# One more half of x convolved on VectorE, and the means of squares on TensorE without column quarters: a change to a convolution, state-space and recurrence kernel

## The chip, the cores and the metric

The kernel runs on one core of one Trainium2 chip. The metric is the device time of one launch in microseconds (us). Before the change three timed runs took 3141.71, 3144.81 and 3148.75 us; the median, 3144.81 us, is the time before. The engines are named as the profile names them: PE is TensorE's matmul, PEld its weight load, DVE is VectorE, ACT is ScalarE, POOL is GpSimd and SP is SyncE, whose queue issues most of the transfers. Each engine works through its own instructions in order.

## The reference, cut to what matters

There are two layers. The first is a group norm, three convolutions and an attention over pixels; the second is a state-space block in two directions over the 4096 tokens of each of four images, followed by a normalized recurrence. The change touches only the state-space block. Cut to that block:

```python
def _mamba3(x, in_proj, conv_w, conv_b, A_log, dt_bias, D, norm_w, out_proj):   # once forwards, once backwards
    zxbcdt = x @ in_proj                                   # 128 channels in
    z, xbc, dt = jnp.split(zxbcdt, [D_INNER, D_INNER + CONV_DIM], axis=-1)   # D_INNER = 256
    xp = jnp.pad(xbc, ((0, 0), (K - 1, 0), (0, 0)))        # K = 4 taps
    conv = sum((xp[:, i:i + l, :] * conv_w[:, i] for i in range(K))) + conv_b
    xbc = jax.nn.silu(conv)
    xh, Bm, Cm = jnp.split(xbc, [D_INNER, D_INNER + D_STATE], axis=-1)
    ...                                                    # dt = softplus(...), A = -exp(A_log)
    y = _ssd(xh, dt, A, Bm, Cm) + xh * D[None, None, :, None]   # chunked scan
    yg = y.reshape(b, l, D_INNER) * jax.nn.silu(z)
    yn = yg * jax.lax.rsqrt(jnp.mean(yg * yg, -1, keepdims=True) + EPS) * norm_w
    return yn @ out_proj
```

So `x` has 256 channels in each of two directions: four halves of 128 channels. Each half needs a projection, a causal convolution over four taps along the tokens, a bias and a SiLU.

## The kernel before

Channels lie on the 128 partitions and tokens along the columns. A *step* n is a chunk of 128 tokens in each direction; four steps make a *group* of 512 tokens; eight groups make an image (a *sequence*), and there are four images: 128 steps, 32 groups. While group G is scanned, the projections of group G+1 are made in between. The instructions of PE and of ACT stand in the order in which the program writes them; those of DVE and POOL are ordered by a scheduler.

A half of x comes about in one of two ways. One projection, then the four taps on ACT (the first) and DVE (the other three):

```python
def project(gr, i, c):                        # direction i, half c
    px = ring.tile([P, MG], F32, tag="big", name="px")       # PSUM, a ring of 3 buffers
    wx = w[1]["x"][:, bass.ts(c, P)] if i else w[0]["x1"]
    nc.tensor.matmul(px, wx, tl[:, rows(g, i, PAD)], start=True, stop=True)              # L1124
    ...
    nc.vector.memset(...)                                                                 # L1128
    nc.scalar.activation(at(0), px, AF.Identity, scale=taps[:, PAD:KC], bias=...)         # L1129
    if g:
        ...  nc.vector.tensor_tensor(v, v, past ..., ALU.add)      # 3 columns, L1133
    for n in range(1, KC):
        nc.vector.scalar_tensor_tensor(at(n), px, taps[...], at(n), ALU.mult, ALU.add)    # L1135

def activate(gr, i, c):
    nc.scalar.activation(x, x, AF.Silu)                                                   # L1139
```

Or four projections, one for each tap with weights that have the tap multiplied in, accumulated in PSUM; only the first half of the forward direction is made so:

```python
def project_fwd(gr):
    px = ring.tile([P, MG], F32, tag="big", name="px")
    for tap in range(KC):
        nc.tensor.matmul(px, w[0]["x"][:, tap, :], tl[:, rows(g, 0, tap)], start=(tap == 0), stop=(tap == KC - 1))  # L1115
    nc.scalar.activation(gr["x"][0][:, 0, :], px, AF.Silu, bias=w[0]["cb"][:, 0:1])       # L1116
```

The means of squares over 256 channels, for the norm at the end, go to two quarters of the array's columns:

```python
def means(gr):                                # QT = 32
    pm = ring.tile([ND * QT, MG], F32, tag="big", name="pm")
    for d in range(ND):
        nc.tensor.matmul(pm[bass.ts(d, QT)], mean, gr["z"][d][:, 0, :], start=True, stop=True,
                         tile_position=(0, d * QT))                                       # L1283
    ms = wk.tile([ND * QT, MG], F32, tag="row", name="ms", bufs=3)
    nc.vector.tensor_scalar(ms, pm, RMS_EPS, None, ALU.add)                               # L1287
    ...
    nc.sync.dma_start(m1..., ms[::QT])        # out to memory, back as columns, rsqrt, spread again
```

One step of the loop, cut to its order (`states` L1212 and L1224, `turn` L1177, `scan` L1234 and L1242, `prepare` L1187 to L1202, `differences` L1168):

```python
for n in range(N):
    G, j = divmod(n, MT)                      # j: 0 to 3 within the group
    S1 = states(m[n], S)                      # PE small L1212, DVE S L1224
    turn(m[n + 1])                            # PE ptr L1177
    scan(m.pop(n), y, S)                      # PE y L1234, L1242
    prepare(m[n + 1])     # PE small L1187, L1189; ACT Exp L1191, copy bt L1193; DVE L1196, gm L1200, lt L1201
    if n % 2: take(gr, j, y)                  # DVE yT L1254
    if j == 0:
        open_group(G + 1); squares(groups[G - 1])
        project(groups[G + 1], 1, 0); project_bc(groups[G + 1], 0); project(groups[G + 1], 0, 1)
    elif j == 1:
        means(groups[G - 1])
        project(groups[G + 1], 1, 1); project_bc(groups[G + 1], 1)     # pb L1103, SiLU L1107
    elif j == 2:
        project_fwd(groups[G + 1])
        for i, c in ((1, 0), (0, 1), (1, 1)): activate(groups[G + 1], i, c)
        for i in range(ND):
            for c in range(2): project_z(gr, i, c)                      # pz L1146, SiLU L1147
        gate(gr, 1)
    elif j == 3:
        gate(gr, 3); back(groups.pop(G - 1))                            # po L1308
    differences(m[n + 2])                     # ACT Relu, 8 times, L1168
    # and, in some steps, pieces of the next image's opening and of the last image's statistics (ls_in L83)
```

Of the kernel before, what the change touches and what calls it, by code (L numbers as in the profile page):

```python
# [10 lines left out]
F32 = mybir.dt.float32  # L11
AF = mybir.ActivationFunctionType
ALU = mybir.AluOpType
# [3 lines left out]
P = 128  # L17
# [9 lines left out]
DS = 64  # L27
DI = NHEAD * HD
KC = 4
GT = NC // P  # L30
DIRS = ("fwd", "bwd")
MG = 512
# [855 lines left out]
def mamba(nc, tc, k, a, t, B, T, vec, first=None, after=None, mr=None):  # L888
# [12 lines left out]
    ND = len(DIRS)  # L901
    HALF = [slice(0, DS), slice(DS, 2 * DS)]
    QT = P // GT

    with ExitStack() as ctx:
# [24 lines left out]
        wp = ctx.enter_context(tc.tile_pool(name="m_w", bufs=1))  # L930
        w = []
        bc_bias, dtb, A = vec["bc_bias"], vec["dtb"], vec["A"]
        wdt = wp.tile([P, QT], F32, name="wdt")
        nc.gpsimd.memset(wdt, 0.0)
        mean = wp.tile([P, QT], F32, name="mean")
        nc.gpsimd.memset(mean, 0.0)
        nc.gpsimd.memset(mean[:, 0:1], 1.0 / DI)
        with tc.tile_pool(name="m_ws", bufs=1) as ws, tc.tile_pool(name="m_wps", bufs=2, space=PSUM) as wps:
            full, cw = [], []
            for i, d in enumerate(DIRS):  # L940
                full.append(ws.tile([P, 2 * DI + 2 * DS + NHEAD], F32, name="full_" + d))
                nc.sync.dma_start(full[i], a[d + "_in_proj"])

                at = DI if i else 0
                cw.append(ws.tile([P, KC, DI + 2 * DS - at], F32, name="cw_" + d))
                nc.scalar.dma_start(
                    cw[i], a[d + "_conv_wt"][:, at:].unsqueeze(0).to_broadcast([P, KC, DI + 2 * DS - at])
                )
            if first is not None:
                scales(0, first)  # L950
            for i, d in enumerate(DIRS):
                centre(nc, k, wps, "c", full[i])
                nc.scalar.copy(wdt[:, bass.ts(i, NHEAD)], full[i][:, 2 * DI + 2 * DS :])
            if first is not None:
                run(scaled(0))
            for i, d in enumerate(DIRS):
                s = dict(taps=vec["taps_" + d], cb=vec["cb_" + d], D=vec["D_" + d])
                w.append(s)
                f = full[i]
                s["z"] = wp.tile([P, DI], F32, name="wz_" + d)  # L960
                s["x"] = wp.tile([P, DI] if i else [P, KC, P], F32, name="wx_" + d)
                s["bc"] = wp.tile([P, KC, 2 * DS], F32, name="wbc_" + d)


                for c in range(KC):
                    nc.vector.tensor_tensor(
                        s["bc"][:, c, :], f[:, 2 * DI : 2 * DI + 2 * DS], cw[i][:, c, -2 * DS :], ALU.mult
                    )
                    if i == 0:
                        nc.gpsimd.tensor_tensor(s["x"][:, c, :], f[:, DI : DI + P], cw[i][:, c, 0:P], ALU.mult)  # L970
                if i:
                    nc.scalar.copy(s["x"], f[:, DI : 2 * DI])
                else:
                    s["x1"] = wp.tile([P, P], F32, name="wx1")
                    nc.scalar.copy(s["x1"], f[:, DI + P : 2 * DI])
                nc.scalar.copy(s["z"], f[:, 0:DI])
            for i, d in enumerate(DIRS):
                out = wp.tile([P, 2, P], F32, name="wout_" + d)
                w[i]["out"] = out
                nc.scalar.dma_start(out, a[d + "_out_proj"].rearrange("(c p) m -> p c m", p=P))  # L980
                for c in range(2):
                    nc.gpsimd.tensor_scalar(out[:, c, :], out[:, c, :], vec["nw_" + d][:, c : c + 1], None, ALU.mult)
# [3 lines left out]
        wk = ctx.enter_context(tc.tile_pool(name="m_wk", bufs=2))  # L986
        ring = ctx.enter_context(tc.tile_pool(name="m_ring", bufs=3, space=PSUM))
# [6 lines left out]
        def rows(g, i, c):  # L994

            return ds(g * MG + c if i == 0 else (NG - 1 - g) * MG + 2 * PAD - c, MG)
# [110 lines left out]
            act = lambda: nc.scalar.activation(gr["bc"][c], pb, AF.Silu, bias=bc_bias[:, c : c + 1])  # L1107
            act() if later is None else later.append(act)

        def project_fwd(gr):  # L1110

            tl, g = gr["tl"], gr["at"][1]
            px = ring.tile([P, MG], F32, tag="big", name="px")
            for tap in range(KC):
                nc.tensor.matmul(px, w[0]["x"][:, tap, :], tl[:, rows(g, 0, tap)], start=(tap == 0), stop=(tap == KC - 1))  # L1115
            nc.scalar.activation(gr["x"][0][:, 0, :], px, AF.Silu, bias=w[0]["cb"][:, 0:1])  # L1116

        def project(gr, i, c):


            tl, g = gr["tl"], gr["at"][1]
            px = ring.tile([P, MG], F32, tag="big", name="px")
            wx = w[1]["x"][:, bass.ts(c, P)] if i else w[0]["x1"]
            nc.tensor.matmul(px, wx, tl[:, rows(g, i, PAD)], start=True, stop=True)  # L1124
            x = gr["x+"][i][:, c, :]
            taps = w[i]["taps"][:, c, :]
            at = lambda n: x[:, PAD - n : PAD - n + MG] if i else x[:, n : n + MG]
            nc.vector.memset(x[:, 0:PAD] if i else x[:, MG:], 0.0)  # L1128
            nc.scalar.activation(at(0), px, AF.Identity, scale=taps[:, PAD:KC], bias=w[i]["cb"][:, c : c + 1])  # L1129
            if g:  # L1130
                v = x[:, MG:] if i else x[:, 0:PAD]
                past = groups[gr["at"][0] * NG + g - 1]["x+"][i][:, c, :]
                nc.vector.tensor_tensor(v, v, past[:, 0:PAD] if i else past[:, MG:], ALU.add)  # L1133
            for n in range(1, KC):
                nc.vector.scalar_tensor_tensor(at(n), px, taps[:, PAD - n : KC - n], at(n), ALU.mult, ALU.add)  # L1135
# [141 lines left out]

        def means(gr):


            pm = ring.tile([ND * QT, MG], F32, tag="big", name="pm")
            for d in range(ND):
                nc.tensor.matmul(  # L1283
                    pm[bass.ts(d, QT)], mean, gr["z"][d][:, 0, :], start=True, stop=True, tile_position=(0, d * QT)
                )
            ms = wk.tile([ND * QT, MG], F32, tag="row", name="ms", bufs=3)
            nc.vector.tensor_scalar(ms, pm, RMS_EPS, None, ALU.add)  # L1287
            n = ND * MG // P
            m1 = dram.tile([P, n], F32, tag="m1", name="m1")
            nc.sync.dma_start(m1.rearrange("(d q) n -> d (q n)", d=ND), ms[::QT])  # L1290
            col = wk.tile([P, n], F32, tag="col", name="col")
            nc.sync.dma_start(col, m1)
            rsqrt(nc, k, col, col)
            m2 = dram.tile([P, n], F32, tag="m2", name="m2")
            nc.sync.dma_start(m2, col)
            gr["rs"] = grp.tile([P, ND, MG], F32, tag="rs", name="rs", bufs=1)
            nc.sync.dma_start(
                gr["rs"].rearrange("p d n -> p (d n)"),
                m2.rearrange("q n -> (q n)").unsqueeze(0).to_broadcast([P, ND * MG]),
            )  # L1300

        STEPS_X = ((1, 0), (0, 1), (1, 1))

        def outputs(gr, d):
            po = ring.tile([P, MG], F32, tag="big", name="po")
# [47 lines left out]
        seqs, groups, m = {}, {}, {}  # L1353
# [42 lines left out]
        open_step(1)  # L1396
        for act in later:
            act()
        project_fwd(groups[0])
        for i, c in STEPS_X:  # L1400
            project(groups[0], i, c)
        differences(m[0])
# [6 lines left out]
        for n in range(N):  # L1409
            G, j = divmod(n, MT)  # L1410
            b, g = divmod(G, NG)
            gr = groups[G]
# [17 lines left out]
            if j == 0:  # L1430
                if more:
                    open_group(G + 1)
                if G > 0:
                    squares(groups[G - 1])
                if more:
                    project(groups[G + 1], *STEPS_X[0])
                if more:
                    project_bc(groups[G + 1], 0)
                if more:
                    project(groups[G + 1], *STEPS_X[1])  # L1440
            elif j == 1:
                if G > 0:
                    means(groups[G - 1])
                if more:
                    project(groups[G + 1], *STEPS_X[2])
                if more:
                    project_bc(groups[G + 1], 1)
            elif j == 2:
                if more:
                    project_fwd(groups[G + 1])  # L1450
                if more:
                    for i, c in STEPS_X:
                        activate(groups[G + 1], i, c)
                for i in range(ND):
                    for c in range(2):
                        project_z(gr, i, c)
                gate(gr, 1)
            elif j == 3:
                gate(gr, 3, not more)
                if not more:  # L1460
                    squares(gr, (0,))
                if G > 0:
                    back(groups.pop(G - 1))
# [293 lines left out]
```

## Time and profile before

| stage | from, us | to, us | what bounds or fills it |
|---|---|---|---|
| convolutions and attention | 0 | about 1695 | PE busy 193 to 196 us in each full 200 us from 200 to 1600 |
| state-space block | about 1695 | about 3000 | PE busy 184 to 193 us of 200, ACT 150 to 168, DVE 136 to 143 |
| recurrence and store | about 3000 | 3147 | a serial chain |

The profiled execution has a span of 3147.0 us. Over it PE is busy for 93% of the time, DVE for 70%, ACT for 58% and POOL for 57%; in the state-space block alone ACT is far higher than its average. The mean granted TensorE clock is 0.977 of full speed.

How it is read: a row of the groups names line, engine, operation, tiles, shapes and count, then the busy time and the mean of one, then the idle time of that engine just before and what ended it. In the timeline a row gives start, duration, instruction and, in brackets, how long its engine had been idle and what released it. One matmul of 32-bit floats appears as two records, two passes over the columns. An engine that is busy all the time is not thereby the one that sets the pace: that is told by the waits, and by what each wait ends on.

### The profile page before, as it was taken

What the parts mean: (1) busy time and instruction counts of PE and PEld (TensorE: products, weight loads), DVE (VectorE), ACT (ScalarE), POOL (GpSimd) and SP (SyncE); (2) the same over time, 40 slices, a digit from 0 to 9 for tenths busy, and PEclk for the clock granted to TensorE, in tenths of its full rate; (3) what the DMA queues carried; (4) which work ended last, traced back from release to release, by engine and by line L of the source; (5) the groups of instructions that cost most, each with busy time, mean ns of one, the idle gap of its engine ahead of it and who ended that gap; (6) DMA issues with size and microseconds to landing.
All of it is one profiled execution on the core that took longest, in us unless ns stands there. A gap on an engine that the chain in (4) does not pass through costs nothing. (4 is left out here: it accounts for less than half of the span.)

```text
span 3147.0 us, 42863 instructions
## 1 busy us (share of the span) xinstructions
PE 2925.4 (93%) x15511; PEld 1458.2 (46%) x15511; DVE 2195.2 (70%) x3429; ACT 1813.8 (58%) x3102; POOL 1798.5 (57%) x1393
## 2 busy tenths in 40 slices
PE   6799999999999999999997999999999999999976
PEld 1344444454444454444453444444444444455545
DVE  7876668666777667687765767776677766777667
ACT  3343434433444434444434878887788778888756
POOL 4258448456584665766553565565555565565644
PEclk9999999999999999999998999999999999999988
DMA  5310101010100101010023343334333343333332
GB/s 181 133 39 30 38 31 45 8 43 23 46 23 30 43 23 38 31 52 33 11 74 92 91 117 95 98 95 115 82 100 94 80 120 89 105 95 103 87 109 109
DMA packets 108394, 224.16 MB, mean 71 GB/s; under 512 B 25678, under 2 KB 29390, under 8 KB 106764
## 3 DMA queue, kind: packets, MB, share of 16 engines
q1 hardware_dynamic: 96588, 177.53, 19.9%
q10 hardware_dynamic: 11584, 43.78, 4.1%
q8 instruction: 125, 2.05, 0.3%
q14 instruction: 97, 0.79, 0.1%
HBM read 200.83 MB, written 20.44 MB: 70 GB/s over the span
## 5 line engine op out<-in xcount | busy, mean ns | idle before, releaser
L477 DVE TENSOR_TENSOR es<-es,ex 128x1024 f32<-128x1024 f32 x448 | 683.2, 1525 | 139.2 <-ACT ex L462 105.8
L462 ACT ACTIVATE ex<-pf 128x1024 f32<-128x1024 f32 x512 | 497.6, 1021 | 464.7 <-PE pf L460 421.2
L460 PE MATMUL pf<-theta,phi 64*128 64x512 f32 x2048 | 513.6, 619 | 20.4 <-ACT ex L462 20.0
L471 PE MATMUL acc<-ex,gT 128*64 128x512 f32 x2048 | 492.8, 607 | 1.7 <-ACT ex L462 1.7
L1202 POOL TENSOR_TENSOR ct<-ct,Cst 128x512 f32<-128x512 f32 x128 | 170.7, 1334 | 343.6 <-DMA ct<-csmem 314.1
L460 PEld LDWEIGHTS pf<-theta,phi 64*128 64x128 f32 x2048 | 173.0, 185 | 340.0 <-ACT ex L462 172.3
L1168 ACT ACTIVATE lt<-lt,cs 128x128 f32<-128x128 f32 x1024 | 312.1, 390 | 0.5 <-DMA lt<-csmem 0.5
L367 PE MATMUL pm<-yf,wt 128*128 128x256 f32 x1152 | 287.1, 382 | 11.9 <-DVE att L483 11.0
L410 ACT ACTIVATE eo<-pm 128x256 f32<-128x256 f32 x88 | 33.7, 383 | 448.9 <-PE pm L367 442.3
L471 PEld LDWEIGHTS acc<-ex,gT 128*64 128x64 f32 x2048 | 127.9, 137 | 339.8 <-issue 327.8
L367 PEld LDWEIGHTS pm<-yf,wt 128*128 128x128 f32 x1152 | 212.9, 189 | 93.4 <-issue 38.7
L1103 PE MATMUL pb<-tl,wbc_fwd 128*64 128x512 f32 x512 | 241.9, 616 | 6.5 <-DVE xT L1135 6.5
L1103 PE MATMUL pb<-tl,wbc_bwd 128*64 128x512 f32 x512 | 242.5, 617 | 0.0
L337 POOL TENSOR_TENSOR yf<-yd 128x272 f32<-128x272 f32 x192 | 234.0, 1246 | 1.4
L1267 POOL TENSOR_TENSOR yT<-yT,zT 128x512 f32<-128x512 f32 x127 | 166.5, 1316 | 58.1 <-DVE yT L1254 50.0
L337 POOL TENSOR_TENSOR yf<-xp 128x272 f32<-128x272 f32 x128 | 108.7, 880 | 136.0 <-PE pm L367 130.2
L1201 DVE TENSOR_TENSOR lt<-lt,gm 128x1024 f32<-128x1024 f32 x128 | 179.2, 1400 | 1.9
L1135 DVE SCALAR_TENSOR_TENSOR xT<-px,taps_bwd,xT 128x512 f32<-128x512 f32 x192 | 143.7, 748 | 8.7 <-ACT xT L1129 4.0
L1234 PE MATMUL y<-lt,xdt 128*64 128x128 f32 x2048 | 142.3, 282 | 7.6 <-PE ptr L1177 3.8
L1221 POOL TENSOR_TENSOR S<-S,tot 128x256 f32<-128x256 f32 x120 | 91.4, 762 | 100.7 <-PE y L1242 91.2
L1103 PEld LDWEIGHTS pb<-tl,wbc_fwd 128*64 128x64 f32 x512 | 66.9, 141 | 174.3 <-issue 142.9
L367 PE MATMUL pm<-yf,wc 128*128 128x256 f32 x512 | 131.3, 384 | 6.6 <-DVE att L483 5.1
(297 smaller groups left out, 5655.5 us busy)
## 6 DMA issues: line engine op xcount, KB each, us to landing
lt<-csmem SPq DMA_DIRECT2D x128, 512.0 KB, 5.7
wt<-wd ACTq DMA_DIRECT2D x72, 576.0 KB, 3.8
ct<-csmem SPq DMA_DIRECT2D x256, 128.0 KB, 5.2
rs<-m SPq DMA_DIRECT2D x31, 512.0 KB, 3.8
wd<-t SPq DMA_DIRECT2D x16, 576.0 KB, 2.8
t<-in_x SPq DMA_DIRECT2D x4, 2048.0 KB, 11.0
rows<-after SPq DMA_DIRECT2D x32, 256.0 KB, 4.4
out<-t SPq DMA_DIRECT2D x4, 2048.0 KB, 14.4
```

What stands on the lines that cost most here:

```text
L337: nc.gpsimd.tensor_tensor(f[:, kx], at(x), at(y), op)
L367: nc.tensor.matmul(pm[:, e, :], wt, src, start=(i == 0), stop=(i == len(terms) - 1))
L460: nc.tensor.matmul(pf[:, e, :], phi[HALF[e], m, :], th[HALF[e]], start=True, stop=True)
L462: nc.scalar.activation(ex, pf, AF.Exp, scale=scale)
L471: nc.tensor.matmul(acc[HALF[e]], gT[:, 2 * m + e, :], ex[:, e, :], start=(m == 0), stop=(m == NT // 2 - 1))
L477: nc.vector.tensor_tensor(es, es, ex, ALU.add)
L1103: nc.tensor.matmul(out, w[i]["bc"][:, tap, bass.ts(c, DS)], src, start=(tap == 0), stop=(tap == KC - 1),)
L1135: nc.vector.scalar_tensor_tensor(at(n), px, taps[:, PAD - n : KC - n], at(n), ALU.mult, ALU.add)
L1168: nc.scalar.activation(v, v, AF.Relu, scale=-1.0, bias=m["b"]["cs"][:, d, m["i"], h : h + 1])
L1201: nc.vector.tensor_tensor(lt, lt, gm.unsqueeze(2).to_broadcast([P, ND, NHEAD, P]), ALU.mult)
L1202: nc.gpsimd.tensor_tensor(m["ct"], m["ct"], Cs[:, cols].unsqueeze(1).to_broadcast([P, NHEAD, P]), ALU.mult)
L1267: eng.tensor_tensor(v, v, gr["z"][d][:, :, half(d, j // 2)], ALU.mult)
```

## The change

The last half of x, the first half of the forward direction, is made like the other three: one projection on PE, the first tap on ACT, three taps on DVE. `project_fwd` and its four sets of weights go; so do the multiplications on POOL that made those weights, and part of a load. The new projection stands at the end of j = 1, so that its SiLU can stand with the other three in j = 2. And the two matmuls of the means no longer lie in two quarters of the columns: they accumulate into the same two rows of PSUM, each with a weight of two columns of which one is zero. The change takes PE work away for the convolution and gives DVE some in its place; the form of the means is simpler, and needs no row stride in the transfer that follows.

```diff
-        mean = wp.tile([P, QT], F32, name="mean")
+        mean = wp.tile([P, ND, ND], F32, name="mean")
         nc.gpsimd.memset(mean, 0.0)
-        nc.gpsimd.memset(mean[:, 0:1], 1.0 / DI)
...
+                nc.gpsimd.memset(mean[:, i, i : i + 1], 1.0 / DI)
-                s["x"] = wp.tile([P, DI] if i else [P, KC, P], F32, name="wx_" + d)
+                s["x"] = wp.tile([P, DI], F32, name="wx_" + d)
...
-                    if i == 0:
-                        nc.gpsimd.tensor_tensor(s["x"][:, c, :], f[:, DI : DI + P], cw[i][:, c, 0:P], ALU.mult)
-                if i:
-                    nc.scalar.copy(s["x"], f[:, DI : 2 * DI])
-                else:
-                    s["x1"] = wp.tile([P, P], F32, name="wx1")
-                    nc.scalar.copy(s["x1"], f[:, DI + P : 2 * DI])
+                nc.scalar.copy(s["x"], f[:, DI : 2 * DI])
...
-        def project_fwd(gr):
-            tl, g = gr["tl"], gr["at"][1]
-            px = ring.tile([P, MG], F32, tag="big", name="px")
-            for tap in range(KC):
-                nc.tensor.matmul(px, w[0]["x"][:, tap, :], tl[:, rows(g, 0, tap)], start=(tap == 0), stop=(tap == KC - 1))
-            nc.scalar.activation(gr["x"][0][:, 0, :], px, AF.Silu, bias=w[0]["cb"][:, 0:1])
...
-            wx = w[1]["x"][:, bass.ts(c, P)] if i else w[0]["x1"]
+            wx = w[i]["x"][:, bass.ts(c, P)]
...
-            pm = ring.tile([ND * QT, MG], F32, tag="big", name="pm")
+            pm = ring.tile([ND, MG], F32, tag="big", name="pm")
             for d in range(ND):
-                nc.tensor.matmul(
-                    pm[bass.ts(d, QT)], mean, gr["z"][d][:, 0, :], start=True, stop=True, tile_position=(0, d * QT)
-                )
-            ms = wk.tile([ND * QT, MG], F32, tag="row", name="ms", bufs=3)
+                nc.tensor.matmul(pm, mean[:, d, :], gr["z"][d][:, 0, :], start=(d == 0), stop=(d == ND - 1))
+            ms = wk.tile([ND, MG], F32, tag="row", name="ms", bufs=3)
...
-        STEPS_X = ((1, 0), (0, 1), (1, 1))
+        STEPS_X = ((1, 0), (0, 1), (1, 1), (0, 0))
...
-        project_fwd(groups[0])
...                                   # j == 1, after project_bc(groups[G + 1], 1)
+                if more:
+                    project(groups[G + 1], *STEPS_X[3])
             elif j == 2:
-                if more:
-                    project_fwd(groups[G + 1])
                 if more:
                     for i, c in STEPS_X:
                         activate(groups[G + 1], i, c)
```

More of the change, by code (lines that the diff above doesn't have):

```diff
@@ L942, in mamba @@
                 nc.sync.dma_start(full[i], a[d + "_in_proj"])
-                at = DI if i else 0
-                cw.append(ws.tile([P, KC, DI + 2 * DS - at], F32, name="cw_" + d))
+                cw.append(ws.tile([P, KC, 2 * DS], F32, name="cw_" + d))
                 nc.scalar.dma_start(
-                    cw[i], a[d + "_conv_wt"][:, at:].unsqueeze(0).to_broadcast([P, KC, DI + 2 * DS - at])
+                    cw[i], a[d + "_conv_wt"][:, DI:].unsqueeze(0).to_broadcast([P, KC, 2 * DS])
                 )
@@ L1289, in means @@
             m1 = dram.tile([P, n], F32, tag="m1", name="m1")
-            nc.sync.dma_start(m1.rearrange("(d q) n -> d (q n)", d=ND), ms[::QT])
+            nc.sync.dma_start(m1.rearrange("(d q) n -> d (q n)", d=ND), ms)
             col = wk.tile([P, n], F32, tag="col", name="col")
```

## The prediction

> **What bounds the kernel now.** I read first where the change lies. The busy time by stretches of 200 us puts the state-space block between about 1695 and 3000 us; nothing the change touches runs before that, so the convolutions and the attention keep their time. Then I took one group of the last image, free of the opening of a next image. A group repeats there every 37.68 us (the Exp of its last step starts at 2795.83 and at 2833.51), and the view of stretches gives its load, in the order PE, PEld, DVE, ACT, POOL, granted clock, DMA share, GB/s:
>
> ```profile
> 2800.00:2837.68 37.68, 37.38 (x264) 19.30 (x263) 27.43 (x64) 31.88 (x64) 22.99 (x19) 1.00 0.37 99
> ```
>
> By this PE is full (99%), ACT at 85% is second, DVE at 73% has room: taking PE work off would seem to be pure gain. That busy share is what misleads here, so I read the chain of waits next. In the group that begins near 2823 us it runs on PE from the means to the first-half projection, then passes to ACT, which lets PE's last projection of z go:
>
> ```profile
> 2823.44 0.98 PE pm L1283 x4
> 2824.42 1.05 PE px L1124 x2
> 2825.48 3.66 PE pb L1103 x16
> ...
> 2833.20 3.65 PE px L1115 x8
> 2836.84 0.02 issue
> 2836.87 0.69 ACT xT L1116
> ...
> 2839.11 0.49 ACT zT L1147
> 2839.61 0.04 issue
> 2839.65 1.13 PE pz L1146 x2
> ```
>
> ACT's timeline for the same stretch shows how much room ACT really has before that point:
>
> ```profile
> 2829.18 0.69 ACT L1107 ACTIVATE Cst<-pb,bc_bias 128x512 f32<-128x512 f32 x1 [1.56 <-PE pb L1103]
> 2829.76 2.44 ACT L1168 ACTIVATE lt<-lt,cs 128x128 f32<-128x128 f32 x8
> 2832.21 1.28 ACT L1191 ACT_TABLE_LOAD   x1
> 2833.51 1.06 ACT L1191 ACTIVATE lt<-lt 128x1024 f32<-128x1024 f32 x1
> 2834.47 0.25 ACT L1193 COPY bt<-small 128x128 f32<-128x128 f32 x1
> 2834.74 1.28 ACT L1116 ACT_TABLE_LOAD   x1
> 2836.87 0.69 ACT L1116 ACTIVATE xT<-px,cb_fwd 128x512 f32<-128x512 f32 x1 [0.85 <-PE px L1115]
> 2837.45 1.66 ACT L1139 ACTIVATE xT<-xT 128x512 f32<-128x512 f32 x3
> 2839.01 1.56 ACT L1147 ACTIVATE zT<-pz 128x512 f32<-128x512 f32 x3
> ```
>
> From the SiLU of C (Cst) on, ACT works without a gap, but for 0.85 us in which it waits for the four-tap projection. So in j = 2 PE has 3.65 us of projection which, if taken away, shortens the path by 0.85 us and no more; after that ACT sets the pace. In a group without a piece of row statistics (ls_in) at the end of j = 1 even that is gone: in the group near 2720 us ACT's table load ended at 2724.04 and its next SiLU began at 2724.15.
>
> **What the Trainium skill says.** "Perfetto Trace Analysis", Identifying the Most-Contended Engine, warns that the busy share of matmuls is no good measure, since they are pipelined. The trace agrees: PE at 37.38 of 37.68 us hides that its four-tap projection lies almost wholly beside ACT work. "TensorEngine Tiling (Array Packing)", Key Properties, says that different tiles of the array can run at once. It agrees: the means before, four passes in two column quarters, take 0.98 us, while two passes of px alone take 1.05. "VectorE: DVE Perf Modes", Why PSUM operands drop a tier, has fp32 operations with a PSUM operand at one element a cycle; the tap on VectorE, 128x512 from PSUM, has a mean of 748 ns and lets the next one start 0.66 us later. "ScalarE: Activation LUTs", What ACT_TABLE_LOAD costs, gives about 1283 ns for a load and the trace has 1.28 us; the further drain of about 1380 ns that it adds does not show here, as the Exp starts at 2833.51 right after the load from 2832.21. The change takes no table load away: the one ahead of L1116 goes to the first of the four SiLUs.
>
> **The change part by part.** One pass over 512 columns costs (3.65 - 1.06) / 6 = 0.43 us, from the eight-record and the two-record projection.
>
> - PE, per group: eight passes become two, 3.65 - 1.06 = 2.6 us less. The means: all four passes go to the same quarter and queue up, 0.98 + 2 x 0.43 = 1.84, so 0.86 us more. Net 1.7 us less; over 31 groups 54 us of busy time.
> - DVE, per group: three taps of 0.66 us and an edge addition of 0.15, 2.1 us more, in j = 1. The row addition on the means costs the same on 2 partitions as on 64, for it goes by its 512 columns.
> - ACT, per group: one more Identity from PSUM (0.68 us until the next instruction starts), and a SiLU that reads from SBUF at 0.52 (three in 1.56) instead of 0.58. Net 0.6 us more.
> - Placement. In ACT's order, which the program fixes, the new Identity stands after the SiLU of C and ahead of the eight Relus. It must wait for its projection, which PE starts only after all of pb.
>
> Now the path anew for the group at 2823 us, in ACT's and PE's order. L1189 ends at 2823.44. Means 1.84: 2825.28. px 1.05: 2826.33. pb 3.66: 2829.99. New px 1.06: 2831.05. Identity starts 0.03 later, and the Relus 0.68 after that: 2831.76. Relus 2.45: 2834.21. Table 1.30: 2835.51. Exp 0.96, copy 0.27: 2836.74. Table 1.30: 2838.04. Four SiLUs of 0.52: 2840.12. The first SiLU of z lets pz go 0.64 after its start, as before (2839.01 to 2839.65): 2840.76 against 2839.65. **The group gets 1.1 us longer**, although PE has 1.7 us less to do: 0.86 of the means lies on the path, the wait for the new projection and its Identity on ACT add more, and of the 2.6 us saved on PE 0.85 comes back. From there on (po, next j = 0) nothing changes.
>
> DVE in that group: the taps of the half (1,1) end by 2830.6, the new taps start after the Identity at 2831.8 and the S of states follows near 2834.5 (2831.51 before). PE's L1187 waits for this S, about where PE arrives anyway (2834.4), and ACT copies bt not before 2836.47, so some 1.6 us are left.
>
> Other groups. Without ls_in at j = 1 the same sum starts from 2711.46 and gives pz at 2728.78 against 2726.93: 1.8 us. Where both the ending and the opening put statistics in j = 1 (group near 2080 us), ACT before waited 2.06 us for px; after, DVE's bn_stats and taps delay S by some 3 us, PE's 3.6 us projection is no longer between S and pz, and I get 0.3. I take 0.3, too, where the opening's softplus work fills DVE. Counting by the program: 12 groups of 1.1, 9 of 1.8, 10 of 0.3, less 0.86 for the first group (no means yet), plus 0.9 for the means of the last loop round: 13.2 + 16.2 + 3.0 + 0 = 32 us. The prologue trades 2.6 us of PE for 2 us of DVE taps, counted as nothing; so does the smaller setup of weights. 3144.8 + 32 = **3177 us**.
>
> **The rivals.** (1) PE is the bound, as its 99% say: 54 us less, about 3091, 1.7% faster. For it: PE shows hardly a gap. Against it: the 0.85 us, and ACT's unbroken run. (2) DVE becomes the bound in j = 1. For it: DVE ran without a gap from 2821.17 to 2833.1, and PE's L1187 already waits for its S (26.4 us in the table of waits). If the 2.1 us come on top of my path in every group, 65 us more, near 3210 to 3240, past the 2%. Against it: DVE is idle for 1.59 and then 5.04 us right after, in j = 2. (3) The change is hidden wholly, as slack elsewhere takes it up: about 3145. For it: ACT waits for PE (2.28 us for L1189) in j = 0. Against it: that wait lies after pz and depends on PE, which comes late by the same amount.
>
> **Range and chances.** The low end, 3154, takes 0.3 us for every group; the high end, 3202, takes 1.8 for all. Rival 1 lies within 2% as well, so faster by over 2% (below 3082) would need more than all PE time saved: 0.03. Slower by over 2% is above 3207.7, rival 2: 0.09. Within 2%: 0.88.
>
> **What would show it.** Means of four records taking 1.8 us on the chain, not 1.0. PE idle some 3 us ahead of the last pz in each group, ended by zT. ACT's gap of 0.85 us gone and a wait of about 1 us ahead of the new Identity. Group spacing in the last image near 38.8 us. PE busy down by about 50 us in all while the span grows. It would be wrong if the two-column weights of the means ran side by side after all, if S on DVE were so late that ACT waits for the copy of bt, or if shorter PE work freed POOL or the transfers of ct somewhere I took as unchanged.

## The result and the profile after

The changed kernel takes 3196.82 us (median; 3188.05 to 3199.23) against 3143.26 us for the kernel before, run with it. The ratio is 1.0163, with a 95% interval of 1.0139 to 1.0186: slower by 1.6%, some 54 us. The prediction had said 3177 us, between 3154 and 3202, and within 2%. The profiled execution is the fastest of the four runs; its span is 3186.0 us, 39 us above the span before, so the trace shows most of the loss and not all of it. Part of the difference lies in the kernel before: its profiled execution, at 3148.75 us, is the slowest of its four.

The view of stretches, for one group of the last image, from one Exp to the same Exp of the next group (columns as in the prediction: PE, PEld, DVE, ACT, POOL, clock, DMA share, GB/s):

```profile
2839.09:2879.04 39.95, 36.96 (x257) 19.14 (x256) 29.69 (x69) 32.69 (x65) 22.48 (x20) 0.96 0.33 93
```

PE has fallen from 37.38 to 36.96 us of busy time, DVE has risen from 27.43 to 29.69, and the group has grown from 37.68 to 39.95 (its three regular neighbours grew by 1.3 to 2.9 us). It is no longer any engine's busy time that fills it. The chain of waits in that group shows who hands over to whom:

```profile
2852.94 0.58 PE small L1196 x4
2853.53 0.59 PE ptr L1161 x4
2854.11 1.02 PE y L1218 x16
...
2856.42 1.81 PE pm L1266 x4
2858.22 1.06 PE px L1108 x2
2859.28 3.60 PE pb L1095 x16
2862.88 1.07 PE px L1108 x2
2863.95 0.02 issue
2863.97 0.78 ACT xT L1113
2864.75 2.33 ACT lt L1152 x8
...
2873.64 1.13 PE pz L1130 x2
2874.76 0.69 PE small L1196 x4
2875.45 1.05 PE ptr L1161 x4
2876.50 1.90 PE y L1218 x16
```

PE leads up to the new projection (px at 2862.88); from 2863.97 on the chain is ACT's until the last z projection at 2873.64. Before the change it was PE's for all but the last 2.8 us of that way. The means take 1.81 us. And a thing I had not foreseen stands in the last three rows: the same work took 0.58, 0.59 and 1.02 us one step earlier (the first three rows), and takes 0.69, 1.05 and 1.90 here. ACT's timeline of the same group:

```profile
2863.97 0.78 ACT L1113 ACTIVATE xT<-px,cb_fwd,taps_fwd 128x512 f32<-128x512 f32 x1 [0.37 <-PE px L1108]
2864.65 2.43 ACT L1152 ACTIVATE lt<-lt,cs 128x128 f32<-128x128 f32 x8
2867.10 1.28 ACT L1175 ACT_TABLE_LOAD   x1
...
2870.92 2.19 ACT L1123 ACTIVATE xT<-xT 128x512 f32<-128x512 f32 x4
2873.01 1.55 ACT L1131 ACTIVATE zT<-pz 128x512 f32<-128x512 f32 x3
```

The gap of 0.85 us ahead of the x SiLUs is gone: ACT works from the Identity on without a pause, and PE waits for it. The table of PE's waits in the state-space block (total, times, longest) has before, then after:

```profile
PE small L1187 <- DVE S L1224: 26.1, 25, 4.2
PE pz L1146 <- ACT zT L1147: 7.5, 31, 0.2
```

```profile
PE pz L1130 <- ACT zT L1131: 73.5, 31, 3.5
PE small L1171 <- DVE S L1208: 43.9, 37, 5.9
```

In each of the 31 groups PE idles ahead of its last z projection, 2.4 us on average in place of 0.24. PE's wait for S, which DVE makes, has grown too, from 26.1 to 43.9 us. In the group shown it is 0.89 us and adds nothing: ACT does not wait for it, and it only takes the place of as much waiting for zT. What comes right behind one of these idles is the view of stretches again, for the 1.9 us of y at 2876.50: PE is busy throughout, at half the clock.

```profile
2876.50:2878.40 1.90, 1.90 (x20) 1.57 (x22) 1.29 (x2) 1.88 (x6) 1.90 (x2) 0.50 0.00 0
```

From the start of the last z projection to the start of y takes over 0.3 us longer than before in 13 of the 31 groups, 15.7 us in all. So there are two losses: a path that goes through ACT, which I had predicted, and a clock that drops behind the idle that this path creates, which I had not.

### The profile page after: what moved, and what is told of

It is laid out like the page before. It is cut to its first block, busy times and chain, and to the rows that moved or that the text cites. A ratio compares the mean times of both kernels' runs of the same rounds, so it can differ in the third digit from the quotient of the medians.

```text
span 3186.0 us, 42657 instructions
## 1 busy us (share of the span) xinstructions
PE 2884.2 (91%) x15319; PEld 1429.8 (45%) x15319; DVE 2278.5 (72%) x3585; ACT 1838.7 (58%) x3134; POOL 1797.2 (56%) x1390
## 3 DMA queue, kind: packets, MB, share of 16 engines
q8 instruction: 123, 2.02, 0.3%
## 4 chain that ended last, share of the span: by engine, by line
PE 67%; DVE 13%; ACT 8%; POOL 5%; issue 3%; DMA 3%; SPq 0%; ACTq 0%; POOLq 0%; DVEq 0%
PE acc L471 13%; PE pf L460 13%; PE pm L367 13%; PE pb L1095 5%; PE px L1108 3%; PE y L1218 2%; PE acc L1559 2%; DVE att L483 2%; DVE xT L1119 2%; PE po L1289 2%; ACT lt L1152 1%; PE pm L1266 1%; PE pz L1130 1%; ACT xT L1123 1%; PE ptr L1161 1%
## 5 line engine op out<-in xcount | busy, mean ns | idle before, releaser
L1119 DVE SCALAR_TENSOR_TENSOR xT<-px,taps_fwd,xT 128x512 f32<-128x512 f32 x192 | 142.2, 741 | 2.5 <-ACT xT L1113 0.5
L1130 PE MATMUL pz<-tl,wz_bwd 128*128 128x512 f32 x128 | 74.3, 664 | 74.8 <-ACT zT L1131 73.8
## 6 DMA issues: line engine op xcount, KB each, us to landing
out<-t SPq DMA_DIRECT2D x4, 2048.0 KB, 14.2
```

## The experiments

Each kernel was timed in rounds with the kernel before on the same chip; the ratios are to that one. The predicted path says that ScalarE's order sets the pace in j = 2 (theory 1). After the trace I added the lowered clock to it. The rivals are VectorE's additional taps (theory 2) and TensorE or the transfers as the bound. The diffs show only the lines that matter.

**The two parts alone.** First the taps on VectorE, with the means still in two quarters:

```diff
-                nc.tensor.matmul(pm, mean[:, d, :], gr["z"][d][:, 0, :], start=(d == 0), stop=(d == ND - 1))
+                nc.tensor.matmul(pm[bass.ts(d, QT)], mean, gr["z"][d][:, 0, :], start=True, stop=True, tile_position=(0, d * QT))
```

> Half (0,0) of x with its taps on VectorE as in the change, but the means still in two column quarters. Theory 1 (in j = 2 ScalarE sets the pace; TensorE then idles ahead of its last z projection, and in the profile of after its clock drops for a few us behind many of these idles): the path per group is 1.1 - 0.86 = 0.25 us longer, 8 us in all, and the idle of 2 to 3.5 us stays, so the clock loss stays with it (some 16 us in the trace of after): about 3167. Theory 2 (VectorE's additional taps delay S and so TensorE): the same taps as after, less 26 us for the means, about 3170, but with TensorE waiting for S or for xT and not for zT. Theory 3 (TensorE is the bound): 80 us less, 3063.

Measured: 3174.69 against 3135.59 us, ratio 1.0125 (1.011 to 1.014), 39 us. The part that I had taken for the cheap one makes most of the loss: 39 us where the path gave 8 and the lowered clock some 16. In the trace the slow stretches are there again, behind 13 of the 31 last z projections, with 17.5 us. In four regular groups of the last image it costs 0.8 to 1.4 us. There the stretch from the Exp made in j = 1 to that made in j = 2 takes 1.15 us longer, and the next one is shorter by 0.75. PE waits 66.3 us for zT and 44.4 us for S.

Then the means alone, in the kernel before:

```diff
-                nc.tensor.matmul(pm[bass.ts(d, QT)], mean, gr["z"][d][:, 0, :], start=True, stop=True, tile_position=(0, d * QT))
+                nc.tensor.matmul(pm, mean[:, d, :], gr["z"][d][:, 0, :], start=(d == 0), stop=(d == ND - 1))
```

> Only the means without column quarters; half (0,0) still by four projections. Theory 1: the four passes queue up, 1.8 us and not 1.0, and all of the 0.86 us lies on the path, 30 times: 26 us, about 3170; TensorE has no idle ahead of the last z projection but the 0.24 us of before, so no clock loss. If two-column weights ran side by side after all: no change, 3144. If the clock loss comes of the means and not of the idle: more than 26 us.

Measured: 3148.28 against 3135.59 us, ratio 1.0036 (1.0022 to 1.005), 13 us: half of what I expected. In the regular groups of the last image the cost is there, 0.76 us in each. In some groups with an image's opening the kernel before is the slower in the traces: the stretch from 2154 to 2172 us has a granted clock of 0.90 before, and means_only passes the same stretch of its program 2.7 us faster. The traces tell what differs there. PE waits 2.02 us for S before, at 2159.58, and 0.91 us in means_only, at 2162.24; the clock drops behind the first and not behind the second.

**The idle filled.** If the lowered clock comes of PE's idle, then work put into that idle must make the kernel faster, though it is of no use:

```diff
-            nc.tensor.matmul(pz, w[i]["z"][:, bass.ts(c, P)], tl[:, rows(g, i, PAD)], start=True, stop=True)
+            for _ in range(3 if (i, c) == (1, 0) else 1):
+                nc.tensor.matmul(pz, w[i]["z"][:, bass.ts(c, P)], tl[:, rows(g, i, PAD)], start=True, stop=True)
```

> The changed kernel, with the third of the four z projections made three times over into the same buffer (same values), so that TensorE works 1.7 us more in each group just where it idled for 1.6 to 3.5 us. Theory 1 with the clock: the slow stretches behind the last z projection go, and the kernel gets faster although it has 53 us more TensorE work: 3197 - 16 to 20, about 3179. If the loss beyond the predicted path has another cause (transfers of ct, VectorE): no gain, 3197 or a few us more, and the slow stretches stay.

Measured: 3175.22 against 3135.59 us, ratio 1.012 (1.0104 to 1.0135), against 1.0163 without the filling. PE's timeline in a group of the last image:

```profile
2867.07 1.13 PE L1131 MATMUL pz<-tl,wz_bwd 128*128 128x512 f32 x2 [0.32 <-ACT zT L1132]
2868.12 0.65 PE L1197 MATMUL small<-xdtd,bt 128*64 128x256 f32 x4
2868.71 0.66 PE L1162 MATMUL ptr<-ident,xT 128*128 128x128 f32 x4
2869.29 1.10 PE L1219 MATMUL y<-lt,xdt 128*64 128x128 f32 x16
```

The idle is 0.32 us, and the three pieces behind it have their full speed back. Four regular groups of the last image now take 1.00, 1.02, 1.01 and 1.03 us more than before; without filling they took 2.93, 1.34, 2.27 and 2.53. That is the predicted path alone (1.1), with the rest gone. Of the slow stretches behind the last z projection none is left in the 31 groups, though PE still idles 1.7 us there in nine of them.

The same filling in taps_only:

> Taps on VectorE with the means in column quarters, and the third z projection made three times over. If the loss of taps_only (39 us) is some 20 us of lowered clock that comes of TensorE's idle, this removes most of it as fill_idle did, though TensorE has 53 us more work: 3135.6 + 20 to 27, about 3159, and (1 - clock) x span falls from 92 to about 76 us. If the loss is VectorE's S alone: no change, 3175.

Measured: 3158.26 against 3140.25 us, ratio 1.0054 (1.0041 to 1.0067). The 39 us have become 18 with 53 us more PE work. In regular groups the cost is 0.4 to 0.8 us; 0.25 was worked out.

And more of it, where an idle of 1.7 us was left (five times over in the groups without row statistics):

> As fill_idle, but five times over in the groups without row statistics at the end of j = 1, whose idle of 3.5 us was filled only to 1.7 us. If what was left of the clock loss lies in these groups: some 3 to 6 us less than fill_idle, about 3171 on the scale of before at 3135.6, and idle ahead of the last z projection below 0.4 us in nearly all groups. If idle of 1.7 us does not lower the clock: the same as fill_idle, 3175.

Measured: 3180.88 against 3140.25 us, ratio 1.0126 (1.0112 to 1.0141), no better than fill_idle. The span's mean clock is 0.977, that of the kernel before, and it is still 1.3% slower. What is left, then, is mostly the path and not the clock. Some of it may be the filling itself: in 12 of the 31 groups it leaves no idle at all ahead of the last z projection, so that it can stand in the way.

**ScalarE relieved.** The first tap of the new half on VectorE, so that ScalarE has neither the Identity nor the wait ahead of its Relus:

```diff
-            nc.scalar.activation(at(0), px, AF.Identity, scale=taps[:, PAD:KC], bias=...)
+            if (i, c) == (0, 0):
+                nc.vector.tensor_scalar(at(0), px, taps[:, PAD:KC], cb, ALU.mult, ALU.add)
+            else: ...   # as it was
```

> The changed kernel, with the first tap of half (0,0) on VectorE as well, so that ScalarE has one Identity less and does not wait for that projection ahead of its Relus. Theory 1 (ScalarE's order sets the pace): the Relus start 1.1 us earlier in each group, about 30 x 1.1 = 33 us less, 3164, as long as VectorE's S does not become the last. Theory 2 (VectorE is the bound): 0.7 us more in each group, about 3218.

Measured: 3175.61 against 3135.59 us, ratio 1.013 (1.0115 to 1.0144). Against the change (1.0163) it gains about 10 us (the intervals of the two ratios still overlap a little) where theory 2 had a loss of some 20, so VectorE was not the bound of the change. It does not gain the 33 us, because VectorE comes next. The chain of waits in a regular group:

```profile
2851.01 0.07 DVE xT L1122
2851.08 0.50 issue
2851.58 0.37 DVE mr L87 x4
2851.95 0.32 DVE S L1211
2852.26 0.04 issue
2852.30 0.33 PE small L1174
2852.63 0.45 PE small L1176 x4
2853.08 0.02 issue
2853.10 0.27 ACT bt L1180
2853.37 0.02 issue
2853.39 1.28 ACT L1126
```

ACT's Exp is early now, but its copy of bt waits for PE, which waits for S, which stands behind the taps (xT) and the row statistics (mr) in VectorE's order. So theory 2 is true one step further on. The 1.6 us that I had left between S and the copy are used up by the earlier ACT and the additional tap. In the four regular groups the cost is 0.8 to 0.9 us, hardly below the 1.0 of the filled change, so the path gained 0.1 to 0.2 us and not 1.1. Most of the 10 us may rather be clock: PE's wait for S takes part of the idle ahead of the last z projection, which is 1.57 us in most groups now, and the slow stretches behind it fall from 13 to 3. No run separates the two.

**Other places for the same work.** The projection, the Identity and the taps behind the Relus, the SiLU of that half behind the first z SiLU, and the means in quarters (the lines for the SiLU and the means are left out):

```diff
                 differences(m[n + 2])
+            if j == 1 and more:
+                project(groups[G + 1], *STEPS_X[3])
```

> An attempt at a version that beats both: means in quarters, half (0,0) by one projection, but its Identity and taps placed behind the eight Relus, and its SiLU behind the first SiLU of z. By the path: ScalarE does not wait for the new projection, and only three SiLUs stand ahead of the z SiLU that releases TensorE: 0.75 us less per group with row statistics, 0.1 more without, about 12 us less in all; the idle ahead of the last z projection stays near 2 us and costs 15 to 20 us of clock: 3135.6 + 3 to 8, about 3142. If VectorE's S is what comes last (it was in taps_only), the gain of the path is lost: about 3160.

> The same with the third z projection made three times over. If the clock follows the idle: 15 us less than without, about 3127, faster than before by 0.3%. If not: no faster than identity_behind_relus.

Measured: 3156.9 against 3140.25 us, ratio 1.0047 (1.0034 to 1.006), and filled 3149.23 us, ratio 1.0029 (1.0018 to 1.0041). The place of that half's projection, Identity, taps and SiLU takes 39 us (taps_only) down to 17. The version was still no gain. PE waits longer for the taps on VectorE than before (pb 14.2 us in place of 6.5, ls_in 6.5 in place of 3.1) and for S (31.0 in place of 26.1); that the half (0,0), a further user of the PSUM ring, is the reason is likely and not shown. The filling is then itself in the way (its twelve z records stand on the chain with 5.49 us), and gains some 8 us and not 15.

Then the projection itself to j = 2, where VectorE was idle for 5 us, and the first z SiLU ahead of all four x SiLUs:

```diff
                 turn(m[n + 1])
+            if j == 2 and G + 1 < NGR:
+                project(groups[G + 1], *STEPS_X[3])
...
                         project_z(gr, i, c)
+                        if more and (i, c) == (0, 0):
+                            for s in STEPS_X: activate(groups[G + 1], *s)
```

> A second attempt at a version that beats both: means in quarters; the new projection of half (0,0) in j = 2 between turn and scan, so that it stands in neither the means-to-C path of j = 1 nor ahead of S; its Identity behind the Relus, its taps where VectorE was idle for 5 us; and the first z SiLU ahead of all four x SiLUs, so that TensorE's last z projection waits for no more than one. By the path: the last z projection starts 2 to 3 us earlier, then TensorE waits some 0.8 us for the x SiLUs ahead of the transposes; ScalarE ends j = 2 about 0.4 us earlier, so 0.4 to 1.1 us less per group, 12 to 34 us in all; the idle becomes shorter than 1.6 us, so that little clock is lost: 3140 - 10 to - 30, about 3120. If ScalarE or VectorE bind elsewhere: 3140 to 3150.

Measured: 3141.93 against 3141.51 us, ratio 1.0002 (0.9994 to 1.001). Moving the half to VectorE, together with the new place of the first z SiLU, costs nothing here, where the move cost 39 us in the other place, but brings none of the 12 to 34 us. What the z SiLU's place alone would bring to the kernel before was not run. PE's longest waits are shared out:

```profile
PE small L1171 <- DVE S L1208: 17.9, 17, 3.3
PE ptr L1161 <- ACT xT L1123: 13.9, 20, 5.3
...
PE pz L1130 <- ACT zT L1131: 11.7, 25, 0.9
```

No single wait is left to take away; groups with one piece of row statistics are 14 us shorter in sum than before, and the other two kinds are 13 us longer.

**A version that is faster than both.** The kernel before, with the SiLU of the four-tap half behind those of the other three (`project_fwd` puts its SiLU into a list for later):

```diff
-                    project_fwd(groups[G + 1])
+                    project_fwd(groups[G + 1], fwd)      # its matmuls; its SiLU goes into fwd
                     for i, c in STEPS_X:
                         activate(groups[G + 1], i, c)
+                    fwd[0]()      # the SiLU of half (0,0)
```

> The kernel before with one thing exchanged: ScalarE does the SiLUs of the other three halves of x while TensorE still makes the four projections of half (0,0), and that half's SiLU after them. If TensorE has only its 0.24 us of idle there, it gains 0.24 us per group at most, about 7 us, 3133. If ScalarE's 0.85 us counted in full on the path: 26 us less, 3114.

Measured: 3128.71 against 3141.51 us, ratio 0.9963 (0.995 to 0.9976): 13 us faster than before. ACT fills its 0.85 us with the SiLUs that are ready:

```profile
2817.05 1.67 ACT L1140 ACTIVATE xT<-xT 128x512 f32<-128x512 f32 x3
2818.63 0.67 ACT L1116 ACTIVATE xT<-px,cb_fwd 128x512 f32<-128x512 f32 x1
```

The regular groups gain 0.46 us and not 0.24: I had counted PE's idle ahead of the last z projection alone; but the last two z projections, from start to the next instruction, take 1.86 us where they took 2.31, so that beside the 0.24 of idle another 0.21 of overlap between them comes back.

## Why the prediction was right

The time lay in the range, and the mechanism is the one told, with one loss missing. That the time lay in the range in spite of this is partly luck: the range was made for the path alone, 32 us, and the missing loss just fitted into its upper half. By the prediction's own steps:

- **ScalarE sets the pace in j = 2, and PE's saving does not count: right.** Ahead of the last z projection PE idles 1.6 to 3.5 us in every group. In the one shown that projection starts 17.22 us after L1173 of j = 1 has ended (2856.42 to 2873.64); the sum had 17.32. The idle is 2.04 us and not 3, as PE had waited 0.9 us for S just before. The wait ahead of the new Identity is 0.37 us and not about 1; the sum itself gave 0.4. PE's busy time is 41 us less over the span (less than 54, as records behind the idle take longer), and the span grows. Rival 1, PE as the bound, is out.
- **The means queue up and lie on the path: right.** 1.81 us for four records, 1.84 predicted; alone they cost 0.76 us in a regular group where I had 0.86. They took 0.83 us more and got 0.06 back, since pb had waited a little for VectorE's taps before. Over all groups the term was too large: 13 us measured for 26. In the traces the kernel before loses clock in some opening groups where means_only does not; whether that makes the whole difference isn't shown.
- **A regular group gets 1.1 us longer: right for the path, too small for the kernel.** Filled, it is 1.02. Unfilled, 1.3 to 2.9.
- **Counted over the groups.** The lengths of the groups, from the Exp of one to that of the next, sum up so, in us more than before:

| kind of group | number | predicted | after | fill_idle |
|---|---|---|---|---|
| no row statistics at j = 1 | 9 | 16.2 | 20.0 | 17.9 |
| one piece of them | 12 | 13.2 | 18.2 | 6.9 |
| VectorE loaded by the opening | 10 | 3.0 | 6.7 | 6.0 |
| sum | 31 | 32.4 | 44.9 | 30.8 |

(The counts are the prediction's. One of the twelve, near 2900 us, has no row statistics either; moved up, it makes 22.2 and 19.7 in the first row, 16.1 and 5.1 in the second.) With the idle filled the sum is near the predicted one; without, 14 us more. The **missing term is the lowered clock**. By the median times the filled kernel is 1.2%, or 38 us, slower than the one before, so 32 us is rather too low for the path even so. And the sum over the kinds agrees better than the kinds, which is luck: the row with one piece is low in fill_idle, where four of its groups got no longer; their clock is 0.93 to 0.96 in the kernel before (2150.6 to 2242.1 and 2485.1 to 2575.2 us) and no lower with the filling, and why the path did not add there stays open.
- **Rival 2, VectorE as the bound: half right.** It did not bind in the change, but stood so close behind ScalarE that relieving ScalarE gained a third of its 33 us at most, and by the regular groups hardly any of it on the path. I had put 9% on it, by an addition of all its time to the path; the true form is that S comes last as soon as ScalarE does not. PE's wait for S in fill_idle is 45.8 us, against 26.1 before; what it adds in the opening groups no run separates from the path.
- **Rival 3, the change hidden wholly: out.** The interval of the ratio begins at 1.0139.
- **The prologue as nothing:** it came out 2.8 us shorter in the trace of after and 0.7 longer in that of fill_idle, which has the same one. That is no more than its spread.
- **Slips of its working.** The four-tap projection did not lie almost wholly beside ACT work: ACT worked or loaded a table in 2.8 of its 3.65 us and waited in the rest, and it is the chain of waits that shows PE as a follower. The high end of the range, 1.8 us for each of 31 groups, is 3201 and not 3202.

Between the traced runs (39 us) and the medians (54 us) 15 us remain. Some 5.5 of them come of the kernel before, whose traced run is that much above its median, and 8.8 of the changed kernel, whose traced run is that much below. Its other runs have a mean clock of 0.967 to 0.969 where the traced one has 0.972, which fits a clock that drops more often; it isn't shown.

## What to carry to other kernels

An engine that is busy for 99% can still be a follower: find the last hand-over in the period (here one z SiLU) and ask how long the other engine was idle ahead of it; that idle, 0.85 us, and not the 2.6 us taken away, is the most that a saving on the busy engine can bring (when it was filled, 0.46 us came back). Where an engine works in order, the place of an added instruction can cost more than the instruction: the same projection, taps and SiLU cost 39 us in one place, 17 in a second, and nothing in a third, where a z SiLU was moved ahead as well. Work taken off an engine can leave an idle behind which its clock drops; ask where the idle will stand. And reordering what is ready ahead of what must be waited for, without any work moved, was the only change here that gained.

## What the runs showed of the hardware that was not expected

TensorE's granted clock dropped to 0.50 for some microseconds behind an idle of about 2 us or more: y took 1.90 us in place of 1.02. It did so in 13 of 31 groups and not in each; one idle of 3.46 us passed without it. Filling the idle with a repeated projection, 53 us of useless work, made the changed kernel about 13 us faster (by the ratios 1.0163 and 1.012) and taps_only 21 us faster (1.0125 and 1.0054). An idle of 0.3 us ahead of the last z projection never brought it in the last image.

What decides whether a given idle is followed by the drop can be read from the traces. In each of them the stretches at 0.50 in the state-space block start whole multiples of 3.413 us apart, as on a fixed grid (2834.16, 2875.12 and 2953.62 us in the changed kernel: 12 and 23 such steps), and last mostly one or two steps. Here are one step of the grid with an idle of 2.04 us and the next step, first for a group with the drop, then for one without it (PE, PEld, DVE, ACT, POOL, clock, DMA share, GB/s):

```profile
2871.71:2875.12 3.41, 1.48 (x6) 0.49 (x6) 0.00 (x0) 3.17 (x7) 0.00 (x0) 1.00 0.67 188
2875.12:2878.53 3.41, 3.41 (x28) 2.49 (x28) 1.71 (x3) 3.39 (x10) 2.47 (x3) 0.50 0.00 0
2793.20:2796.61 3.41, 1.94 (x9) 0.80 (x10) 0.11 (x1) 3.17 (x7) 0.00 (x0) 1.00 0.60 157
2796.61:2800.02 3.41, 3.41 (x45) 2.58 (x44) 1.60 (x3) 3.39 (x9) 2.81 (x3) 1.00 0.16 47
```

The idle is as long in both. In the first group nearly all of it (1.93 us) falls into one step; in the second 0.57 us falls into the step before, and 1.47 us are left. Counted from the first Exp to the last in all twelve traces, a step at full clock was followed by one at 0.50 in 135 of 140 cases where PE had been idle for 1.8 us or more of it, in 21 of 142 between 1.4 and 1.8 us, and in none of 3966 below 1.4 us. So an idle of 1.57 us brought no drop behind the last z projection, and one of 3.46 us can escape it where the grid cuts it nearly in half (1.68 and 1.78 us in the group near 2078 us). This is read from the runs; no run shifted the grid on purpose.
